# Decoder kernel on one core: reciprocal softmax sums transposed by DMA in 16-bit planes instead of on TensorE, and transposes moved in the slot order

## The chip, the core and the metric

The kernel runs on one core of one Trainium2 chip. The metric is the device time of one execution in microseconds; of three runs before the change the median is 2231.85 us (2231.59 to 2232.89). The trace comes from one further execution, taken with the hardware profiler.

The engines are named as the profile names them: PE is TensorE (PEld its weight loads), DVE is VectorE, ACT is ScalarE, POOL is GpSimd, SP is the queue from which nearly all DMAs are issued. Each engine executes its own instructions in order.

## What is computed

A decoder layer with post-norm, on 32 batches of 256 tokens by 256 features, all in float32 except the feed-forward matmuls. Cut to what matters here:

```python
x = layernorm(x + self_attn(x))          # 16 heads of 64, 4 KV heads, rope, alibi
x = layernorm(x + cross_attn(x, ctx))    # 16 heads of 16, windows of 64 keys, mask by cell
x = layernorm(x + ffn(x))                # 1024 wide, ternary weights, 8-bit activations

# inside self_attn
attn = softmax(q @ k.T / 8 + alibi)      # per head, 256 x 256
out  = (attn @ v).transpose(...).reshape(b, l, 16 * 64)
return out @ Wo
```

The change is inside the softmax of the self attention: its division by the row sums.

## The kernel before

**The unit of work.** One batch is cut into eight units of self scores (`self_units`: query half `qc`, KV half `kc`, head pair `rp`); two units make a pair, numbered m, with four pairs to a batch. A pair covers 128 queries and eight heads. For a pair:

- `self_scores` (L392, L408): PE writes scores to PSUM, DVE adds alibi, writes `p` and the row minimum `nm`.
- `self_exp` (L426): ACT takes exponentials in place and accumulates the row sums in `sums`, a [128 queries x 8 heads] tile.
- `self_turn` (L453, L458): PE transposes `p` in 128x128 blocks (as a matmul with `ident`), ACT copies them to `pT`.
- `self_values` (L470, L477): PE multiplies `v` with `pT`. The result `oT` has the 64 features of two heads on the partitions and the queries along the free axis; ACT copies it to SBUF. It is not normalized yet.
- `self_inverse` (L439, L441): DVE takes the reciprocals of `sums` and writes each one 64 times side by side in `wide`, [128 queries x 8 heads x 64].
- `self_spread` (L485): PE transposes `wide` in four 128x128 blocks to a PSUM bank `R`, so that each reciprocal stands on the 64 partitions of its head, over the queries.
- `self_normal` (L493): DVE multiplies `oT` by `R`.
- `self_output` (L501 and what follows): the output projection `wo`, the residual and the first layer norm, and the queries of the cross attention.

The cross attention has four units to a batch: `cross_scores` (L662, L676), `cross_exp` (L692), `cross_turn` (L701, L703: transposes `xp` on PE, ACT copies them to `xpT`), `cross_values` (L717, L726), `cross_back` (L737, L742, L743). The feed-forward has its own generator (L804 to L855).

**The order.** A hand-written schedule fixes the order on PE, DVE and ACT. Time is cut in slots, four to a pair: slot = 4m + part. In each slot the loop at the end of the kernel emits fixed pieces, and `parts()` emits the next piece of every generator that is due (projections of the coming batch, output projections, feed-forward, cross inputs). The cross attention runs CROSS = 4 pairs behind (k = m - 4). The order on SP and POOL isn't written by hand: the framework's scheduler places their instructions. In the text Q0, Q1, Q2 and Q3 are the four pairs m = 4b to 4b + 3 of a batch. The output projection of the first query half falls in Q2 (parts 1 and 2), that of the second in Q0; the feed-forward's gate matmuls fall in Q3 (parts 2 and 3), its up matmuls in Q0, its down matmuls in Q2.

**Buffers.** PSUM is a ring of eight banks (`bank`), taken in the order of the code; a matmul group waits until the bank that it takes, eight allocations back, has been read. SBUF tiles are taken from rings by name (`work(name, shape, bufs)`). SP's DMAs wait, in order, for their data: a DMA whose data is late holds those behind it. The DMAs on SP are rope's half swaps (`other<-psin`, `other<-qb`), loads of `xT`, `xs`, `cs`, `ck_i`, copies to `kTz` and `xvaug`, the store `out_dram<-x`, and the feed-forward's transposing DMAs `xiT` and `hiT` on bf16 data.

Of the kernel before, what the change touches and what calls it, by code (L numbers as in the profile page):

```python
# [9 lines left out]
F32 = mybir.dt.float32  # L10
BF16 = mybir.dt.bfloat16
I32 = mybir.dt.int32
AF = mybir.ActivationFunctionType
ALU = mybir.AluOpType
AX = mybir.AxisListType

P = 128
L = 256
NT = L // P
D = 256  # L20
NDC = D // P
# [4 lines left out]
H, KV, HD = 16, 4, 64  # L26
NCH = H // 2
# [23 lines left out]
def kernel(  # L51
# [27 lines left out]
    nc = tc.nc  # L79
# [5 lines left out]
    def ctile(shape, dtype, name):  # L85
        return const.tile(shape, dtype, name=name, tag=name)
# [3 lines left out]
    def bank(name, shape=(P, 512), dtype=F32):  # L90
        return ps.tile(list(shape), dtype, tag="b", name=name)


    ident = ctile([P, P], F32, "ident")
# [7 lines left out]
    def work(name, shape, bufs=2, dtype=F32):  # L102
        return sb.tile(list(shape), dtype, tag=name, name=name, bufs=bufs)

    def small(name, n):
        return sb.tile([P, 8], F32, tag="small", name=name, bufs=48)[:, 0:n]
# [21 lines left out]
    nc.scalar.dma_start(base_sb, mask_base)  # L128
    cq_i = ctile([P, B, NT], I32, "cq_i")
    nc.scalar.dma_start(cq_i, cell_q)  # L130
# [60 lines left out]
    def flush():  # L191
        while last:
            last.pop(0)()

    def scaled(dst, src, rb):

        nc.scalar.activation(dst, src, AF.Identity, bias=rb[:, 1:2], scale=rb[:, 0:1])

# [221 lines left out]
    def self_exp(b, i, half):  # L420
        s = state[b]
        p, nm = s["p", i][half], s.pop(("nm", i, half))
        for rr in range(2):
# [4 lines left out]
                p[:, cols],  # L428
                AF.Exp,
                bias=nm[:, rr : rr + 1],  # L430
# [3 lines left out]

    def self_inverse(b, m):

        s = state[b]
        rinv = small("rinv", 8)
        nc.vector.reciprocal(rinv, s.pop(("sums", m)))  # L439
        s["rinv", m] = wide = work("wide", [P, 8, HD], 1)  # L440
        nc.vector.tensor_copy(wide, rinv.unsqueeze(2).to_broadcast([P, 8, HD]))  # L441

    def self_turn(b, i):
        s = state[b]
# [31 lines left out]
                    )  # L476
        nc.scalar.copy(oT.rearrange("p c t -> p (c t)"), po)  # L477

    def self_spread(b, m):

        s = state[b]
        wide = s.pop(("rinv", m))
        s["R", m] = pr = bank("R")
        for r in range(NCH // 2):
            nc.tensor.transpose(  # L485
                pr[:, r * P : (r + 1) * P], wide[:, 2 * r : 2 * r + 2, :].rearrange("p a e -> p (a e)"), ident
            )

    def self_normal(b, m):
        s = state[b]  # L490
        qc, kc, _rp = self_units[2 * m]
        oT = s["oT", qc, kc].rearrange("p c t -> p (c t)")
        nc.vector.tensor_tensor(oT, oT, s.pop(("R", m)), ALU.mult)  # L493

    def self_output(b, qc):

        s = state[b]
        py = bank("wo")
        for kc in range(2):
            for r in range(NCH // 2):  # L500
                nc.tensor.matmul(  # L501
                    py[:, 0:D],
                    s["oT", qc, kc][:, r, :],
                    wo_sb[:, 4 * kc + r, :],
                    start=(kc == 0 and r == 0),
                    stop=(kc == 1 and r == 3),
                )
            if kc == 0:
                yield
        h = work("row", [P, D], 6)  # L510
        nc.vector.tensor_tensor(h, py[:, 0:D], s["xs"][:, qc, :], ALU.add)
        mv = stats(h, "x1")


        rs = small("rs_x1", 3)
        nc.gpsimd.tensor_scalar(rs[:, 0:1], mv[:, 1:2], EPS, None, ALU.add)
        nc.gpsimd.tensor_scalar(rs[:, 1:2], mv[:, 1:2], 1.0 + EPS, EPS * EPS, ALU.mult, ALU.add)
        nc.gpsimd.tensor_tensor(rs[:, 0:2], rs[:, 0:2], neg_half, ALU.pow)
        nc.gpsimd.tensor_scalar(rs[:, 2:3], mv[:, 0:1], rs[:, 0:1], -1.0, ALU.mult, ALU.mult)
        yield  # L520
        zq = work("row", [P, D], 6)

        s["x1", qc] = x1 = work("x1", [P, D], 4)

        def residual():
            nc.vector.tensor_scalar(zq, h, mv[:, 0:1], rs[:, 1:2], ALU.subtract, ALU.mult)
            nc.scalar.activation(x1, h, AF.Identity, bias=rs[:, 2:3], scale=rs[:, 0:1])
            nc.gpsimd.tensor_tensor(x1, x1, xbias[O_], ALU.add)

        last.append(residual)  # L530
        yield
        zqT = work("zT", [P, NDC, P])
        transposed(zqT, zq, "zqT")
        yield 2
        pq = bank("xq")
        for ch in range(NDC):
            for dc in range(NDC):
                nc.tensor.matmul(  # L538
                    pq[:, ch * P : (ch + 1) * P],
                    xq_w[:, dc, ch * P : (ch + 1) * P],  # L540
                    zqT[:, dc, :],
                    start=(dc == 0),
                    stop=(dc == NDC - 1),
                )
        s["xqT", qc] = work("xqT", [P, NDC, P])
        pair = biased(pq, Q_, P)
        yield 2
        rotated(s["xqT", qc], *pair, 0, qc * P)


    def biased(pq, j, n):


        qb = work("qb", [P, 2 * L])[:, 0 : NDC * n]
        for ch in range(NDC):
            nc.scalar.activation(
                qb[:, ch * n : (ch + 1) * n], pq[:, ch * n : (ch + 1) * n], AF.Identity, bias=xbcol[j][:, ch : ch + 1]
            )
        other = work("other", [P, 512], 3)[:, 0 : NDC * n]
        for e in range(2):  # L560
            nc.sync.dma_start(other[e : P : 2, :], qb[1 - e : P : 2, :])
        return qb, other
# [13 lines left out]
    def cross_inputs(b):  # L576
# [3 lines left out]
        nc.sync.dma_start(cs, cx[b].rearrange("(t p) d -> p t d", p=P))  # L580
        ck_i = work("ck_i", [P, L], 1, I32)
        nc.sync.dma_start(ck_i, cell_k[b].partition_broadcast(P))
# [104 lines left out]
    def cross_exp(b, i, half):  # L687
        s = state[b]
        p = s["xp", i, half]
        for j in range(XHH):  # L690
            cols = slice(j * P, (j + 1) * P)
            nc.scalar.activation(  # L692
                p[:, cols], p[:, cols], AF.Exp, bias=s["xnm", i][half][:, j : j + 1], scale=-1.0
            )
# [79 lines left out]
    def feed_forward(b):  # L774
# [39 lines left out]
        for t in range(NT):  # L814
            for half in range(2):
                pg = hidden("gate", t, half)
                cols = gu[:, t, half * 512 : (half + 1) * 512]
                nc.scalar.activation(cols, pg, AF.Tanh, scale=g_of[:, t : t + 1])  # L818
                nc.vector.scalar_tensor_tensor(cols, cols, 1.0, pg, ALU.add, ALU.mult)  # L819
# [48 lines left out]
    state = {b: {} for b in range(B)}  # L868
# [19 lines left out]
    with tc.manual_schedule(engines={mybir.EngineType.PE, mybir.EngineType.DVE, mybir.EngineType.Activation}):  # L888
        running = []
        slot = min(starts)  # L890
        while starts or running:
            m, part = divmod(slot, 4)
            k = m - CROSS
            for gen in starts.pop(slot, ()):
                running.append([slot, gen])

            def cross(f, unit, *more):
                if 0 <= unit < 4 * B:
                    f(*divmod(unit, 4), *more)

            def pair(f, unit):
                if 0 <= unit < 4 * B:
                    f(*divmod(unit, 4))

            def own(f, unit, *more):
                if 0 <= unit < 8 * B:
                    f(*divmod(unit, 8), *more)

            def parts():
                for r in list(running):  # L910
                    if r[0] == slot:
                        wait = next(r[1], r)
                        if wait is r:
                            running.remove(r)
                        else:
                            r[0] += wait or 1

            if part == 0:
                own(self_scores, 2 * m)
                own(self_scores, 2 * m + 1)  # L920
                own(self_exp, 2 * m, 0)
                own(self_exp, 2 * m, 1)
                own(self_exp, 2 * m + 1, 0)
                pair(self_values, m - 1)
                own(self_exp, 2 * m + 1, 1)
                pair(self_spread, m - 1)
                parts()
                pair(self_normal, m - 1)
                cross(cross_turn, k - 1, 0)
                cross(cross_turn, k - 1, 1)  # L930
            elif part == 1:
                parts()
                cross(cross_scores, k)
                cross(cross_values, k - 1)
                cross(cross_exp, k, 0)
            elif part == 2:
                parts()
                cross(cross_exp, k, 1)
                own(self_turn, 2 * m)
                cross(cross_back, k - 1)  # L940
            else:
                pair(self_inverse, m)
                parts()
                own(self_turn, 2 * m + 1)
            flush()
            slot += 1

# [88 lines left out]
```

## Time and profile before

| what | value |
|---|---|
| median of three runs | 2231.85 us |
| the profiled execution | 2230.19 us |
| its span | 2228.4 us |
| mean granted PE clock over the span | 0.986 |
| instructions | 55216 |
| DMA: bytes moved, mean | 144.05 MB, 65 GB/s |
| SP queue (q1), share of the 16 DMA engines' time | 24.6% |

The span is the profiled stretch; 1.8 us lie around it. The engine rows give busy time as a share of the span. A matmul's end is modelled, and matmuls overlap, so PE's busy share hides short waits: they are better seen from the starts of successive groups in the timeline. One batch is one period of the steady state; in the middle of the trace it lasts 66.48 us, from one start of Q0's value matmuls (1011.96 us) to the next (1078.44 us). Four stretches of this period begin with the value matmuls of a pair: Q0 at 1011.96, Q1 at 1026.95, Q2 at 1042.11, Q3 at 1064.06.

### The profile page before, as it was taken

How to read it: one execution, taken by the hardware profiler on the slowest of the kernel's cores; microseconds unless marked ns; L12 is line 12 of the kernel's file. 1: busy time of each engine (PE TensorE's matmuls, PEld its weight loads, DVE VectorE, ACT ScalarE, POOL GpSimd, SP SyncE). 2: the span in 40 equal slices, each digit the busy share in tenths (PEclk: the TensorE clock that was granted, in tenths of full speed). 3: DMA queues.
4: the chain of work that ended last, by engine and by line, in shares of the span. 5: the costliest groups of instructions: out<-in, count | busy, mean ns of one | idle time of the engine just before them, and what ended most of it. 6: DMA issues, size and time to landing. Idle time of an engine off the chain costs nothing.

```text
span 2228.4 us, 55216 instructions
## 1 busy us (share of the span) xinstructions
PE 2148.1 (96%) x17828; PEld 1672.0 (75%) x17828; DVE 1740.1 (78%) x6949; ACT 1678.0 (75%) x4961; POOL 1106.4 (50%) x1849
## 2 busy tenths in 40 slices
PE   7899999999999999999999999999999999999974
PEld 5687777777777777777777777777777777777752
DVE  4777888878887877887877887887788887888775
ACT  2577778887778877778787777887877887777862
POOL 4344554545554545544545544545555445555442
PEclk8999999999999999999999999999999999999996
DMA  6322222222222223222222322222222222222111
GB/s 206 94 57 56 69 55 63 62 56 70 70 54 62 64 55 73 68 57 63 61 58 70 69 59 58 60 64 65 70 66 53 66 58 63 70 63 49 34 41 31
DMA packets 191424, 144.05 MB, mean 65 GB/s; under 512 B 107808, under 2 KB 160928, under 8 KB 191136
## 3 DMA queue, kind: packets, MB, share of 16 engines
q1 hardware_dynamic: 189440, 136.95, 24.6%
q8 instruction: 142, 2.33, 0.5%
q10 hardware_dynamic: 1696, 3.57, 0.4%
q14 instruction: 146, 1.20, 0.2%
HBM read 39.50 MB, written 8.39 MB: 21 GB/s over the span
## 4 chain that ended last, share of the span: by engine, by line
PE 72%; DVE 11%; ACT 9%; issue 3%; DMA 2%; POOL 1%; SPq 1%; ACTq 0%; DVEq 0%; POOLq 0%
PE wo L501 10%; PE o L470 9%; PE proj L329 8%; PE t L453 8%; PE s L392 6%; PE ff L804 5%; ACT p L426 4%; PE xt L701 4%; PE xo L717 3%; PE xq L538 3%; PE xs L662 3%; PE ffo L851 3%; PE R L485 3%; PE xk L610 3%; PE xw L763 2%
## 5 line engine op out<-in xcount | busy, mean ns | idle before, releaser
L426 ACT ACTIVATE p<-p,nm 128x256 f32<-128x256 f32 x1024 | 507.3, 497 | 89.5 <-DVE nm L408 89.5
L458 ACT COPY pT<-t 128x512 f32<-128x512 f32 x512 | 275.9, 597 | 149.0 <-PE t L453 148.3
L408 DVE CUSTOM_DVE_ANT_0 p<-s,alibi 128x256 f32<-128x256 f32 x1024 | 361.9, 417 | 5.0 <-PE s L392 4.9
L692 ACT ACTIVATE xp<-xp,xnm 128x128 f32<-128x128 f32 x1024 | 327.2, 397 | 25.7 <-DVE xnm L676 25.7
L676 DVE CUSTOM_DVE_ANT_0 xp<-xs,mask 128x128 f32<-128x128 f32 x1024 | 225.8, 286 | 82.4 <-PE xs L662 82.1
L453 PE MATMUL t<-ident,p 128*128 128x128 f32 x2048 | 266.8, 273 | 0.9 <-ACT p L426 0.9
L470 PE MATMUL o<-pT,v 128*64 128x256 f32 x2048 | 261.0, 386 | 3.9 <-ACT pT L458 0.9
L453 PEld LDWEIGHTS t<-ident,p 128*128 128x128 f32 x2048 | 238.0, 141 | 27.0 <-ACT p L426 2.6
L353 POOL TENSOR_TENSOR qT<-qT,other 128x512 f32<-128x512 f32 x128 | 163.8, 1279 | 188.4 <-DMA other<-psin 138.7
L392 PE MATMUL s<-kT,qT 64*128 64x256 f32 x2048 | 255.7, 389 | 0.0
L329 PE MATMUL proj<-xT,wq_sb 128*128 128x256 f32 x1024 | 246.4, 385 | 0.0
L501 PE MATMUL wo<-wo_sb,oT 128*128 128x256 f32 x1024 | 245.3, 383 | 0.0
L470 PEld LDWEIGHTS o<-pT,v 128*64 128x64 f32 x2048 | 144.3, 136 | 106.7 <-issue 21.2
L392 PEld LDWEIGHTS s<-kT,qT 64*128 64x128 f32 x2048 | 187.9, 186 | 38.0 <-issue 16.1
L501 PEld LDWEIGHTS wo<-wo_sb,oT 128*128 128x128 f32 x1024 | 191.5, 192 | 27.0 <-DVE gu L297 0.3
L329 PEld LDWEIGHTS proj<-xT,wq_sb 128*128 128x128 f32 x1024 | 188.1, 193 | 21.7
L426 ACT ACTIVATION_READ_ACCUMULATOR p<-p,nm 128x1 f32 x1024 | 192.4, 188 | 0.0
L493 DVE TENSOR_TENSOR oT<-oT,R 128x512 f32<-128x512 f32 x128 | 86.9, 679 | 114.2 <-ACT oT L477 104.2
L840 POOL TENSOR_SCALAR gu<-gu,ffhup 128x1024 f32<-128x1024 f32 x64 | 72.8, 1137 | 161.3 <-DVE ffhup L836 161.3
L819 DVE SCALAR_TENSOR_TENSOR gu<-gu,ff 128x512 f32<-128x512 f32 x128 | 82.5, 684 | 77.2 <-ACT gu L818 77.2
L726 ACT COPY xoT<-xo 128x256 f32<-128x256 f32 x128 | 47.6, 372 | 124.9 <-PE xo L717 123.3
L600 POOL TENSOR_SCALAR mask<-ck_i,cq_sb 64x128 f32<-64x128 f32 (+1 forms) x96 | 70.2, 731 | 141.3 <-DVE xnm L676 135.3
(148 smaller groups left out, 4579.9 us busy)
## 6 DMA issues: line engine op xcount, KB each, us to landing
other<-psin SPq DMA_DIRECT2D x640, 64.0 KB, 2.0
xT<-in_xt_dram SPq DMA_DIRECT2D x32, 256.0 KB, 2.7
xs<-in_x_dram SPq DMA_DIRECT2D x32, 256.0 KB, 2.7
cs<-in_ctx_dram SPq DMA_DIRECT2D x32, 256.0 KB, 2.9
other<-qb SPq DMA_DIRECT2D x64, 128.0 KB, 2.0
kTz<-tr SPq DMA_DIRECT2D x256, 32.0 KB, 2.0
other<-qb SPq DMA_DIRECT2D x128, 64.0 KB, 1.9
out_dram<-x SPq DMA_DIRECT2D x32, 256.0 KB, 2.3
```

Of the source, the lines that this page charges most:

```text
L329: nc.tensor.matmul(pq[:, c * L : (c + 1) * L], w[:, dc, c * P : (c + 1) * P], xT[:, dc, :], start=(dc == 0), stop=(dc == NDC - 1),)
L353: nc.gpsimd.tensor_tensor(d2, d2, other, ALU.add)
L392: nc.tensor.matmul(banks[half][:, rr * L : (rr + 1) * L], qT[rows_, rr, qc * P : (qc + 1) * P], kT[rows_, kc, :], start=(rr == 0), stop=(r ...
L408: nc.vector.tensor_tensor_reduce(p[:, cols], banks[half][:, cols], alibi[:, 2 * (4 * kc + 2 * rp + rr) + half, :], -0.125, 3.0e38, ALU.add ...
L426: nc.scalar.activation(p[:, cols], p[:, cols], AF.Exp, bias=nm[:, rr : rr + 1], scale=-1.0, accum_out=s["sums", i // 2][:, e : e + 1],)
L453: nc.tensor.transpose(pt[:, j * P : (j + 1) * P], p[half][:, rr * L + kk * P : rr * L + (kk + 1) * P], ident,)
L458: nc.scalar.copy(pT[half], pt)
L470: nc.tensor.matmul(po[half * HD : (half + 1) * HD, rp * L : (rp + 1) * L], s["v"][:, kk, (2 * kc + half) * HD : (2 * kc + half + 1) * HD], ...
L501: nc.tensor.matmul(py[:, 0:D], s["oT", qc, kc][:, r, :], wo_sb[:, 4 * kc + r, :], start=(kc == 0 and r == 0), stop=(kc == 1 and r == 3),)
L676: nc.vector.tensor_tensor_reduce(p[:, cols], banks[2 * half + j // 2][:, j % 2 * P : (j % 2 + 1) * P], s["mask"][:, qc, :], -1.0, 3.0e38, ...
L692: nc.scalar.activation(p[:, cols], p[:, cols], AF.Exp, bias=s["xnm", i][half][:, j : j + 1], scale=-1.0)
L804: nc.tensor.matmul(pg, xiT[:, t, dc, :], ff_w[name][:, dc, half * 512 : (half + 1) * 512], start=(dc == 0), stop=(dc == NDC - 1),)
```

## The change

The reciprocals' transposition leaves PE. `self_inverse` now writes the reciprocals as 16-bit halves: a float32 is read as two uint16, and `wide` becomes [128, 2 planes, 8 heads, 64] uint16 (1024 elements for 512 before, the same bytes). A transposing DMA on SP, of 16-bit elements, turns it to `planes`. A new `self_spread` has POOL interleave the two planes back into float32 in an SBUF tile `R`; `self_normal` is unchanged in code but reads `R` from SBUF rather than PSUM. To make room, four rings are shortened: `row` from 6 to 4, `x1` from 4 to 3, `qb` from 2 to 1, and the new tiles have one buffer each.

The slot order changes too: `cross_turn` goes from the end of part 0 to directly behind `self_values`; `self_inverse` goes from the head of part 3 to part 2, ahead of `cross_exp(k, 1)` and `cross_back`; in part 3 `self_turn(2m + 1)` goes ahead of `parts()`; `self_spread` goes from part 0 of the next pair to the end of part 3.

```diff
     def self_inverse(b, m):
         s = state[b]
         rinv = small("rinv", 8)
         nc.vector.reciprocal(rinv, s.pop(("sums", m)))
-        s["rinv", m] = wide = work("wide", [P, 8, HD], 1)
-        nc.vector.tensor_copy(wide, rinv.unsqueeze(2).to_broadcast([P, 8, HD]))
+        wide = work("wide", [P, 2, 8, HD], 1, U16)
+        nc.vector.tensor_copy(
+            wide,
+            rinv.bitcast(U16).rearrange("p (a z) -> p z a", z=2).unsqueeze(3).to_broadcast([P, 2, 8, HD]),
+        )
+        s["planes", m] = planes = work("planes", [P, 2, NCH // 2, P], 1, U16)
+        nc.sync.dma_start_transpose(
+            planes.rearrange("p z r q -> p (z r) q"), wide.rearrange("p z a e -> p (z a e)")
+        )
+
+    def self_spread(b, m):
+        s = state[b]
+        s["R", m] = R = work("R", [P, 512], 1)
+        nc.gpsimd.tensor_copy(
+            R.bitcast(U16).rearrange("p (n z) -> p z n", z=2),
+            s.pop(("planes", m)).rearrange("p z r q -> p z (r q)"),
+        )
...
-    def self_spread(b, m):
-        s = state[b]
-        wide = s.pop(("rinv", m))
-        s["R", m] = pr = bank("R")
-        for r in range(NCH // 2):
-            nc.tensor.transpose(
-                pr[:, r * P : (r + 1) * P], wide[:, 2 * r : 2 * r + 2, :].rearrange("p a e -> p (a e)"), ident
-            )
...
-        h = work("row", [P, D], 6)
+        h = work("row", [P, D], 4)
...
-        zq = work("row", [P, D], 6)
-        s["x1", qc] = x1 = work("x1", [P, D], 4)
+        zq = work("row", [P, D], 4)
+        s["x1", qc] = x1 = work("x1", [P, D], 3)
...
-        qb = work("qb", [P, 2 * L])[:, 0 : NDC * n]
+        qb = work("qb", [P, 2 * L], 1)[:, 0 : NDC * n]
...
             if part == 0:
...
                 pair(self_values, m - 1)
+                cross(cross_turn, k - 1, 0)
+                cross(cross_turn, k - 1, 1)
                 own(self_exp, 2 * m + 1, 1)
-                pair(self_spread, m - 1)
                 parts()
                 pair(self_normal, m - 1)
-                cross(cross_turn, k - 1, 0)
-                cross(cross_turn, k - 1, 1)
...
             elif part == 2:
                 parts()
+                pair(self_inverse, m)
                 cross(cross_exp, k, 1)
                 own(self_turn, 2 * m)
                 cross(cross_back, k - 1)
             else:
-                pair(self_inverse, m)
+                own(self_turn, 2 * m + 1)
                 parts()
-                own(self_turn, 2 * m + 1)
+                pair(self_spread, m)
```

More of the change, by code (lines that the diff above doesn't have):

```diff
@@ L12 @@
 I32 = mybir.dt.int32
+U16 = mybir.dt.uint16
 AF = mybir.ActivationFunctionType
```

## The prediction

> **What bounds the kernel now.** I read the page first: engine shares, slices and the chain that ended last.
>
> ```profile
> PE 2148.1 (96%) x17828; PEld 1672.0 (75%) x17828; DVE 1740.1 (78%) x6949; ACT 1678.0 (75%) x4961; POOL 1106.4 (50%) x1849
> ...
> PE   7899999999999999999999999999999999999974
> ...
> PE 72%; DVE 11%; ACT 9%; issue 3%; DMA 2%; POOL 1%; SPq 1%; ACTq 0%; DVEq 0%; POOLq 0%
> ```
>
> PE is nearly always busy, and POOL half idle, so taking work from PE and giving it to POOL looks right. But a fifth of the chain is on DVE and ACT: in places PE is not the limit. Second, the timelines of one period, first PE, then ACT and DVE around the start of Q0:
>
> ```profile
> 1009.85 2.00 PE L392 MATMUL s<-kT,qT 64*128 64x256 f32 x16
> 1011.96 2.33 PE L470 MATMUL o<-pT,v 128*64 128x256 f32 x16
> 1014.22 0.66 PE L485 MATMUL R<-ident,wide 128*128 128x128 f32 x4
> 1014.71 1.03 PE L763 MATMUL xw<-xo_w,zT 128*128 128x256 f32 x4
> ...
> 1026.95 1.95 PE L470 MATMUL o<-pT,v 128*64 128x256 f32 x16
> ```
>
> ```profile
> 1009.51 1.09 ACT L458 COPY pT<-t 128x512 f32<-128x512 f32 x2
> 1010.45 1.31 ACT L818 ACTIVATE gu<-ff,ffg 128x512 f32<-128x512 f32 x2
> 1011.60 1.12 ACT L458 COPY pT<-t 128x512 f32<-128x512 f32 x2
> 1012.94 0.51 ACT L426 ACTIVATE p<-p,nm 128x256 f32<-128x256 f32 x1 [0.22 <-DVE nm L408]
> ```
>
> ```profile
> 1011.22 1.28 DVE L819 SCALAR_TENSOR_TENSOR gu<-gu,ff 128x512 f32<-128x512 f32 x2 [0.50 <-ACT gu L818]
> ```
>
> In Q1 and Q2 each PE group starts where the last ends: `o` takes 1.95 us. From Q3 to the start of Q0 ACT works without a gap, and PE waits for it: `o` in Q0 takes 2.33 us and starts 0.17 us after `s` has let go (1009.85 + 1.93 = 1011.79), about 0.55 us lost. Busy times by stretch agree: ACT is busy 13.20 of Q3's 14.38 us, but 12.04 of Q0's 14.99.
>
> **The change, part by part.**
>
> *R leaves PE.* A run of eight transposes lasts 0.87 us in the chain of waits, so four cost 0.44 us. The R group holds PE 0.49 us to the next start, and 0.59 in the chain; the rest is a pause at the change from 64-column to 128-column weights (the weight loads of R sit idle 0.38 us before it, put down to issue), which the next 128-column group, `xt`, will pay instead. So 128 pairs x 0.44 = 56 us of PE time go; upper end 128 x 0.59 = 76.
>
> *DVE's `wide`.* The row of before, and those that price its successor:
>
> ```profile
> L441 DVE COPY wide<-rinv 128x512 f32<-128x512 f32 x128 | 84.9, 664 | 4.4
> L843 DVE TENSOR_SCALAR hib<-gu 128x1024 bf16<-128x1024 f32 x64 | 44.3, 693 | 10.1 <-POOL gu L840 10.1
> ```
>
> Now 1024 elements are written for 512. `hib` writes 1024 in 0.69 us; the old `wide` takes 0.43 undisturbed (426 ns its minimum). I take 0.69, +0.27 a pair; lowest +0 (all halves packed), highest +0.8, from the 1024-element reduction L831 at 1.21 us. DVE has room except before `s` in Q3, below. `oT` times R (0.69 us) keeps its size; reading R from SBUF may make it wait for POOL, as `wide` does (up to 1532 ns): between 0 and +0.8, taken 0.
>
> *The transposing DMA.* It has the size and form of `hiT`:
>
> ```profile
> hiT<-hib SPq DMA_TRANSPOSE x64, 3.1
> ```
>
> so 1.28 us on SP and 3.1 us to landing, 128 times: 164 us more of SP, which idles much. Here a rule speaks against the change: the Trainium skill, "VectorE: DVE Perf Modes", section "The three transpose paths", gives 390 ns for a 128x128 16-bit block on TensorE and 1309 ns by DMA, and its rules keep TensorE wherever PSUM output will do. Estimated from that page, four blocks (1.56 us) are exchanged for eight (10.5 us), a clear loss. The rows are far from both: 0.44 us of PE for 3.1 us of latency. What decides is that the one is PE's time and the other only delay, if R still arrives.
>
> *POOL's spread.* 1024 two-byte elements, one input. Nearest row: the same operation on `ck_i`, 256 elements in 0.40 us; with the slope of one-input work on POOL (L840, 1024 elements, 1.14; L791, 256, 0.48: 0.86 ns an element) that gives 1.06 us. Upper end: the slowest one-input row of POOL, L223 at 922 ns for 256, would make 3.7. I take 1.1 (nearest in kind). It adds 136 us to POOL's 1106.
>
> *Does R come in time?* On SP and POOL the new order sets it. Each case starts from `wide`, in times of before, and ends at L493, which can't start before ACT's copy of `oT`:
> - Q0's (wide 1024.5): SP idle, landed 1027.7; POOL has `x1` and half of `rstd_zo` ahead (1027.5); R at 1028.8, L493 at 1030.6.
> - Q1's (1040.8 to 1041.2): landed 1044.5; POOL first finishes `xqT` (1045.5); R 1046.6, L493 1047.7.
> - Q2's (1060.4): its DMA now stands behind the store `out_dram`, which waits for ACT's last `x` (1062.8 before, about 1060 once the fourth slot's transposes come first); landed 1064; POOL ends rope and `x1` at 1065.3; R 1066.4, L493 1068.8.
> - Q3's (about 1076.5): the DMA is put between the `kTz` copies, landed 1079.6; R 1080.7, L493 about 1083.
>
> So R is 1.1 to 2.4 us early. Behind Q3's DMA wait five `kTz` copies (0.67 us each, 2.0 to landing): done near 1083, and `xs` of Q0 needs them at 1084.2. Behind Q1's stand the second `hiT` and rope swaps, used some 8 us later or about 1 us late for POOL, which has nothing urgent there. `rstd_zo` behind R comes 1.1 us later, used by ACT 4 us on.
>
> *Head.* In the first pair POOL's R stands behind `ck_i` and the mask (done 50.3 us), while L493 ran at 47.1: DVE waits 4.3 us. It idles 6.3 us at 60 to 66, waiting in the end for ACT and POOL, so part is absorbed: cost 0 to 4, taken 2.
>
> *`cross_turn` earlier.* ACT now makes the `xpT` copies ahead of two exponentials (2 x 0.49) and `zT` (0.25): `xo` gets its data 1.2 us sooner, `zT` comes at the time of the old `xpT`; `xq`, behind `xo`, then waits for that in Q3. *Fourth slot's transposes earlier.* PE no longer waits at Q0's `o`: gain 0.55 at that place. But in Q3 ACT's second pair of tanh now follows both copies, so DVE's `gu` and the scores behind it come later. *Rings.* `qb` is read by POOL to 1064.6, its next writer is at 1072.9; 1045.5 against 1055.1 in the other case; `row` and `x1` turn over slots apart: no cost. If POOL were 8 us late, ACT would stand at `qb`.
>
> *Sum for one batch.* The path that sets Q3 and Q0: `wo` ends at 1056.8 on PE, DVE works without a gap to the scores of Q3, ACT starts its exponentials at 1065.19 and goes on to Q0's `xo` (1085.4). On it: wide +0.27; behind the copies, tanh to 1079.5, `gu` and one score to 1080.6, so exponentials 1.2 later than 1079.4; then six instead of eight of them ahead of `xpT`: -0.98. `xpT` is ready at 1085.1, `xo` gains 0.3 us where PE alone would gain 1.9. Q1 and Q2 are bound by PE and gain 0.44 each. Together 1.2 us x 32 batches = 38 us; head +2. Profiled execution: 2230.2 (span 2228.4 and 1.8 around it) - 36 = 2194; the median stands 1.7 above it: **2195 us**.
>
> **The rivals.**
> - *PE sets the whole period.* For it: 96% busy, no visible wait in most groups; if DVE's scores in Q3 aren't held by `gu` the 56 us are all real, and with the 0.55 at Q0's `o` (18 us): 2232 - 72 = 2160. Against: ACT's unbroken row from Q3 on.
> - *R comes too late: slower.* Place: L493, in order on DVE, with the whole of part 1 behind it. Price: if POOL's spread takes t, R misses L493 in Q1 from t = 2.2 us on, in Q0 from 2.9, in Q2 from 3.4. At the upper end of 3.7 these are 1.5, 0.8 and 0.3, 2.6 us a batch on DVE; less the 1.2 gained, 1.4 x 32 = 45: about 2277. The sign turns near t = 3.1. Against it: no one-input row of POOL in the steady state is that slow for its size. A `kTz` landing late at Q0's `xs` is milder, 1 us x 32, and would leave 2227.
> - *Nothing moves.* The pause at the weight change and ACT's path eat the gain: within 5 us.
>
> **Chances and range.** Likeliest (2180 to 2215): 0.48. PE-bound (2150 to 2180): 0.26. Nothing: 0.06. Slower: 0.20. A measurement of this kernel tells 0.2% (4.5 us) from no change. Faster 0.74, same 0.06, slower 0.20. The range 2152 to 2245 leaves out the larger part of the slower case and the tail of the faster one; the likeliest's own is 2180 to 2215.
>
> **What would show it.** No L485; `wide` near 690 ns; a DMA row `planes` near 3.1 us; the POOL copy near 1.1 us; L493 still waiting for ACT's `oT`, not for POOL. A period of about 65.3 us, `xo` of Q0 waiting for `xpT`, and ACT waiting over 1 us at Q0's first exponential. Wrong if L493 waits for POOL's R in most pairs, if `xs` waits for `kTz`, or if POOL's copy is above 2.2 us.

## The result, and the profile after

After the change the median of four runs is **2210.83 us** (2209.87 to 2211.08), beside 2231.72 us of four runs before (2230.14 to 2232.89): a ratio of **0.9906** [0.9889, 0.9923], 20.9 us less. The profiled execution took 2211.1 us, with a span of 2209.3 us at a mean granted clock of 0.980 (0.986 before; the undisturbed PE groups keep their times, `wo` 1.73 us in both).

From the page of the changed kernel, busy times and the chain that ended last:

```profile
PE 2103.3 (95%) x17254; PEld 1617.7 (73%) x17316; DVE 1789.9 (81%) x6949; ACT 1659.5 (75%) x4961; POOL 1316.8 (60%) x1977
...
PE 58%; DVE 20%; ACT 12%; DMA 3%; issue 2%; POOL 1%; SPq 0%; ACTq 0%; POOLq 0%; DVEq 0%
```

PE does 44.8 us less, but the span is only 19.1 us shorter. PE's share of the chain fell from 72 to 58%, DVE's rose from 11 to 20%, ACT's from 9 to 12%: where PE made room, the other two now end last. The view of waits names the places (total us, times, longest):

```profile
ACT p L427 <- DVE nm L409: 235.8, 94, 21.9
...
DVE oT L500 <- ACT oT L494: 110.2, 120, 2.8
...
PEld xq L545 <- ACT zT L205: 51.6, 63, 1.1
...
PE xq L545 <- ACT zT L205: 37.8, 61, 0.8
...
DVE oT L500 <- POOL R L455: 9.6, 3, 4.5
```

ACT's exponentials on the page of before, with 89.5 us of waiting ahead of them:

```profile
L426 ACT ACTIVATE p<-p,nm 128x256 f32<-128x256 f32 x1024 | 507.3, 497 | 89.5 <-DVE nm L408 89.5
```

ACT waits 235.8 us for DVE's scores, where it waited 89.5 us before. The wait of `xq` for `zT` is new: 61 times, two a batch. `oT` times `R` still waits for ACT's `oT`; for POOL's `R` it does so only three times, two of them in the first 200 us (7.9 us, the longest 4.5).

The timeline of PE (start, us) from Q3 to Q1 of one batch:

```profile
993.95 1.42 PE L669 MATMUL xs<-kTz,xqT 32*64 32x256 f32 x16
995.30 0.79 PE L724 MATMUL xo<-xpT,xvaug 128*32 128x64 f32 x32
996.92 1.16 PE L545 MATMUL xq<-zT,xq_w 128*128 128x128 f32 x8 [0.82 <-ACT zT L205]
...
1001.91 2.49 PE L393 MATMUL s<-kT,qT 64*128 64x256 f32 x16
1004.33 1.95 PE L487 MATMUL o<-pT,v 128*64 128x256 f32 x16
...
1024.00 0.64 PE L724 MATMUL xo<-xpT,xvaug 128*32 128x128 f32 x16
1025.06 1.16 PE L545 MATMUL xq<-zT,xq_w 128*128 128x128 f32 x8 [0.41 <-ACT zT L205]
```

Before, in Q1:

```profile
1032.88 0.64 PE L717 MATMUL xo<-xpT,xvaug 128*32 128x128 f32 x16
1033.46 1.16 PE L538 MATMUL xq<-zT,xq_w 128*128 128x128 f32 x8
```

No `R` stands between `o` and `xt` any more, and `o` of Q0 takes 1.95 instead of 2.33 us. Three things are longer: `xq` in Q3 stands 0.82 us, `s` of Q0 takes 2.49 instead of 2.00, and `xq` in Q1, which followed `xo` at once before, stands 0.41 us. A busy row of digits hides all three. To sum them, take the time from one PE group's start to the next, averaged over 20 batches in the middle of the run (us; four of the experiments below stand beside it). `s` of Q0 is the score group ahead of Q0's `o`:

| step of PE | before | after | moves alone (e3) | e3 without `R` (e5) | 512 float32 `wide` (e9) | 1024 16-bit `wide` (e10) |
|---|---|---|---|---|---|---|
| `R` and `xt`, four pairs | 5.46 | 3.72 | 5.47 | 3.72 | 3.72 | 3.72 |
| Q3: `xs` | 1.13 | 1.02 | 0.72 | 0.75 | 0.72 | 0.94 |
| Q3: `xo`, up to `xq` | 0.84 | 1.61 | 1.05 | 1.55 | 1.51 | 1.61 |
| Q0: `s` | 2.10 | 2.42 | 2.04 | 2.04 | 2.42 | 2.42 |
| Q0: `o` | 2.26 | 1.88 | 1.88 | 1.88 | 1.88 | 1.88 |
| Q0: `xs` and `xo` | 1.23 | 1.24 | 1.24 | 1.63 | 1.24 | 1.24 |
| Q1: `xo`, up to `xq` | 0.57 | 1.06 | 0.57 | 0.64 | 0.81 | 1.07 |
| period of a batch | 66.45 | 65.85 | 65.86 | 65.11 | 65.16 | 65.78 |

From before to after: -1.74 for `R`, -0.11, +0.77, +0.32, -0.38 and +0.49 in the rows below it, together -0.65, and 0.05 more at Q2's `xs`; the period fell by 0.60, and 32 x 0.60 = 19 us. So of 1.74 us that left PE in each batch, about 1.1 came back: at `xq` as waits for ACT's `zT`, at `s` of Q0 in part as waits for ACT's `pT` (29 waits of its weight loads, one in nearly every batch).

The pieces of the transport, by form (busy us, mean ns | idle us before, releaser), and its DMA beside one of the same form:

```profile
L455 POOL COPY R<-planes 128x1024 uint16<-128x1024 uint16 x128 | 173.5, 1356 | 21.9 <-DMA planes<-wide 21.6
...
L443 DVE COPY wide<-rinv 128x1024 uint16<-128x1024 uint16 x128 | 108.2, 845 | 4.5 <-DVE rinv L441 0.2
...
L533 DVE TENSOR_SCALAR row<-row,mv_x,rs_x 128x256 f32<-128x256 f32 x64 | 50.3, 785 | 1.2 <-POOL rs_x L525 1.1
```

```profile
planes<-wide SPq DMA_TRANSPOSE x128, 3.1
...
hiT<-hib SPq DMA_TRANSPOSE x64, 3.1
```

`wide` is 693 ns at its least, 798 in the median and 1445 at its longest. The DMA lands after 3.1 us, as its neighbour does. `row<-row`, which the change doesn't touch, has a mean of 0.82 us in the middle of the run, against 0.60 before: this row is the clue to what follows.

### The profile page after: what moved, and what is told of

Read it like the earlier page. It is cut to its first block, busy times and chain, and to the rows that moved or that the text cites. A ratio compares the mean times of both kernels' runs of the same rounds, so it can differ in the third digit from the quotient of the medians.

```text
span 2209.3 us, 54605 instructions
## 1 busy us (share of the span) xinstructions
PE 2103.3 (95%) x17254; PEld 1617.7 (73%) x17316; DVE 1789.9 (81%) x6949; ACT 1659.5 (75%) x4961; POOL 1316.8 (60%) x1977
## 3 DMA queue, kind: packets, MB, share of 16 engines
q8 instruction: 138, 2.26, 0.4%
q14 instruction: 150, 1.23, 0.2%
## 4 chain that ended last, share of the span: by engine, by line
PE 58%; DVE 20%; ACT 12%; DMA 3%; issue 2%; POOL 1%; SPq 0%; ACTq 0%; POOLq 0%; DVEq 0%
PE wo L508 9%; PE t L470 8%; DVE p L409 7%; PE s L393 6%; ACT p L427 6%; PE o L487 5%; PE proj L330 5%; PE ff L811 4%; PE xq L545 3%; PE xt L708 3%; ACT xpT L710 3%; PE ffo L858 3%; PE xk L617 2%; PE xw L770 2%; PE v L362 2%; DMA out_dram<-x 2%
## 5 line engine op out<-in xcount | busy, mean ns | idle before, releaser
L427 ACT ACTIVATE p<-p,nm 128x256 f32<-128x256 f32 x1024 | 508.3, 499 | 235.8 <-DVE nm L409 235.8
L393 PE MATMUL s<-kT,qT 64*128 64x256 f32 x2048 | 271.4, 392 | 0.0
L475 ACT COPY pT<-t 128x512 f32<-128x512 f32 x512 | 263.7, 598 | 7.0 <-PE t L470 6.8
L354 POOL TENSOR_TENSOR qT<-qT,other 128x512 f32<-128x512 f32 x128 | 178.7, 1396 | 137.9 <-DMA other<-psin 113.1
L487 PE MATMUL o<-pT,v 128*64 128x256 f32 x2048 | 249.8, 386 | 0.0
L393 PEld LDWEIGHTS s<-kT,qT 64*128 64x128 f32 x2048 | 197.5, 187 | 68.6 <-issue 16.2
L487 PEld LDWEIGHTS o<-pT,v 128*64 128x64 f32 x2048 | 136.4, 137 | 98.1 <-issue 42.3
L500 DVE TENSOR_TENSOR oT<-oT,R 128x512 f32<-128x512 f32 x128 | 98.0, 765 | 119.8 <-ACT oT L494 110.2
L455 POOL COPY R<-planes 128x1024 uint16<-128x1024 uint16 x128 | 173.5, 1356 | 21.9 <-DMA planes<-wide 21.6
L847 POOL TENSOR_SCALAR gu<-gu,ffhup 128x1024 f32<-128x1024 f32 x64 | 73.5, 1149 | 143.9 <-DVE ffhup L843 143.9
L708 PEld LDWEIGHTS xt<-ident,xp 128*128 128x128 f32 x1024 | 112.1, 143 | 49.0 <-issue 36.2
```

What stands on the lines that cost most here:

```text
L354: nc.gpsimd.tensor_tensor(d2, d2, other, ALU.add)
L393: nc.tensor.matmul(banks[half][:, rr * L : (rr + 1) * L], qT[rows_, rr, qc * P : (qc + 1) * P], kT[rows_, kc, :], start=(rr == 0), stop=(r ...
L427: nc.scalar.activation(p[:, cols], p[:, cols], AF.Exp, bias=nm[:, rr : rr + 1], scale=-1.0, accum_out=s["sums", i // 2][:, e : e + 1],)
L475: nc.scalar.copy(pT[half], pt)
L487: nc.tensor.matmul(po[half * HD : (half + 1) * HD, rp * L : (rp + 1) * L], s["v"][:, kk, (2 * kc + half) * HD : (2 * kc + half + 1) * HD], ...
L708: nc.tensor.transpose(pt[:, j * P : (j + 1) * P], p[:, j * P : (j + 1) * P], ident)
```

## The experiments

The theory to be tested (A) is this: from Q3 to Q0 ACT's row of work, fed by DVE's scores, sets the time, so time won on PE there returns as a wait. Against it: PE still sets the period and one of the moves does harm; or a part of the transport, `wide`, the DMA or POOL's copy, costs the time. All ratios are to the kernel before, run on the same chip.

| run | what | us | ratio [95%] | period, us |
|---|---|---|---|---|
| e1_cross_back | after, `cross_turn` at its old place | 2257.33 | 1.0104 [1.0089, 1.0120] | 67.29 |
| e2_turn_back | after, fourth slot's `self_turn` at its old place | 2204.53 | 0.9866 [0.9852, 0.9881] | 65.55 |
| e3_moves_only | before, with both moves; `R` stays on PE | 2208.06 | 0.9880 [0.9865, 0.9895] | 65.86 |
| e4_parts_first | after, `parts()` of part 0 ahead of `cross_turn` | 2206.96 | 0.9875 [0.9858, 0.9891] | 65.59 |
| e5_no_r_moved | e3 without `R` | 2185.81 | 0.9799 [0.9785, 0.9814] | 65.11 |
| e6_no_r_before | before without `R` | 2203.51 | 0.9878 [0.9863, 0.9893] | 65.53 |
| e7_no_pool_copy | after without POOL's copy | 2207.30 | 0.9898 [0.9881, 0.9914] | 65.78 |
| e8_cross_only | before, with the move of `cross_turn` alone | 2224.55 | 0.9970 [0.9959, 0.9981] | 66.37 |
| e9_wide32_early | after without DMA and copy, `wide` in float32 | 2190.70 | 0.9804 [0.9788, 0.9819] | 65.16 |
| e10_wide16_only | e9 with the 16-bit `wide` | 2208.50 | 0.9888 [0.9874, 0.9903] | 65.78 |
| e11_r_on_pe_parts_first | e3 with `R` and `parts()` ahead of `cross_turn` | 2208.41 | 0.9889 [0.9872, 0.9905] | 65.81 |
| e12_turn_back_parts_first | after with the edits of e2 and e4 | 2207.46 | 0.9883 [0.9868, 0.9897] | 65.63 |

The medians of before beside them were 2233.53 (e1 to e4), 2230.67 (e5 to e8) and 2232.09 us (e9 to e12). e5, e6, e7, e9 and e10 multiply `oT` by ones in place of `R`, so the softmax isn't normalized in them; DVE's multiplication keeps its size, but not its time: its mean over the 20 batches is 0.81 us in e5 and 0.84 in e6, beside 0.69 in e3 and 0.68 before; in e7, e9 and e10 it is 0.73, beside 0.75 in after.

**The move of `cross_turn`, undone and alone.** e1, against after:

```diff
                 pair(self_values, m - 1)
-                cross(cross_turn, k - 1, 0)
-                cross(cross_turn, k - 1, 1)
                 own(self_exp, 2 * m + 1, 1)
                 parts()
                 pair(self_normal, m - 1)
+                cross(cross_turn, k - 1, 0)
+                cross(cross_turn, k - 1, 1)
```

> The changed kernel with cross_turn back at the end of part 0. In the changed kernel the query matmuls xq wait for ACT's zT copy in Q1 (0.49 us a batch) and Q3 (0.77). Theory A (ACT's row from the scores on is the limit; the order only chooses which copy is last): xpT becomes the last copy, xo waits in place of xq, and xq, which follows xo, starts some 0.3 us later in each of the two: period 66.2 to 66.5 us, time 2217 to 2232. Theory B (the waits are made by the move of cross_turn alone): both waits go, period 64.6 us, time near 2171.

Measured: 1% slower than before, 67.29 us a batch, worse than either theory had it, although nothing stands on PE for `R`. Its PE timeline, `xo` of Q3, Q0 and Q1:

```profile
1014.10 0.91 PE L724 MATMUL xo<-xpT,xvaug 128*32 128x64 f32 x32 [1.06 <-ACT xpT L710]
...
1029.05 0.91 PE L724 MATMUL xo<-xpT,xvaug 128*32 128x64 f32 x32 [0.62 <-ACT xpT L710]
...
1043.43 0.91 PE L724 MATMUL xo<-xpT,xvaug 128*32 128x128 f32 x16 [0.52 <-ACT xpT L710]
```

`xo` waits three times in each batch for copies that ACT makes behind all eight exponentials. So this move is no ornament: beside the rest of the change the old place of `cross_turn` costs 1.44 us a batch (65.85 to 67.29). It isn't `R`'s absence alone that makes it so dear: e6 below, the old order throughout without `R`, is faster than before.

e8 makes the same move in the kernel before, and nothing else:

> The kernel before with one move alone: cross_turn directly behind self_values; R stays on PE, the fourth slot keeps its order. If the gain of the change is this move: period 65.5 to 65.9, time 2197 to 2210. If it needs R off PE or the other move: 66.2 or more, 2222 or more.

It gains 0.3%, some 6 us, as if the move needed `R` off PE or the other move. `xo` is free and `xs` in Q3 0.46 us shorter, but the step from `xo` to `xq` is 0.19 longer (1.03), `s` of Q0 takes 2.29 us (2.10 before), and `o` keeps its 2.26.

**Both moves, with `R` left on PE.** e3, against before:

```diff
                 pair(self_values, m - 1)
+                cross(cross_turn, k - 1, 0)
+                cross(cross_turn, k - 1, 1)
                 own(self_exp, 2 * m + 1, 1)
...
-                cross(cross_turn, k - 1, 0)
-                cross(cross_turn, k - 1, 1)
...
                 pair(self_inverse, m)
-                parts()
                 own(self_turn, 2 * m + 1)
+                parts()
```

> The kernel before, with R on PE, and only the two moves: cross_turn directly behind self_values, fourth slot's transposes ahead of parts(). Theory A: the moves trade the waits at xo and o (0.26 and 0.55 us a batch) for one at xq (0.4 to 0.8): period 66.2 to 66.5, time 2223 to 2234. Theory D (the moves are worth what the forecast gave them, 0.5 us or more a batch): time 2212 or less.

Both moves are `cross_turn`'s and the fourth slot's; `self_inverse` stays where it was. Measured: 0.9880, and the period of the whole change to 0.01 us; that is theory D's outcome, not A's. So the two moves alone bring what the change brings, with 1.75 us of `R` still on PE. The table has both columns: after has no `R`, and pays 0.30 and 0.56 in Q3, 0.38 at `s` of Q0 and 0.49 in Q1, together 1.73.

**`R` taken away for nothing.** e5 removes `R` from e3, without a transport; e6 removes it from before. The edit in both:

```diff
-        nc.vector.tensor_tensor(oT, oT, s.pop(("R", m)), ALU.mult)
+        o3 = s["oT", qc, kc]
+        nc.vector.tensor_tensor(o3, o3, ones.unsqueeze(1).to_broadcast([P, NCH // 2, P]), ALU.mult)
...
-                pair(self_spread, m - 1)
```

> Both moves on the kernel before, R nowhere: wide is written in float32 as before, PE's four transposes of it are left out, there is no DMA and no POOL copy, and oT is multiplied by ones (the normalization is left out). Theory H (PE's time under R lies beside ACT and DVE, which set the end; leaving it out makes PE wait longer): period 65.4 to 65.9, time 2195 to 2210, waits at xo, xq and Q0's s larger than with R on PE by about what went. Theory T (R's place on PE is worth 1.7 us a batch and the transport gives it back through DVE and POOL): period 64.1 to 64.6, time 2155 to 2172.

> The kernel before in its own order, R nowhere: as the run above but without the moves (the normalization is left out). Theory H: xpT is the last copy of ACT's row and PE now waits for it at xo in Q3, Q0 and Q1; period 65.9 to 66.4, time 2215 to 2230. Theory T: period 64.7, time near 2176.

In the moved order the period falls by 0.75 us (65.86 to 65.11), in the old order by 0.92 (66.45 to 65.53), where PE loses some 1.7 us of work. Both lie between the two theories: of PE's 56 us, 24 to 29 came out by the periods (18 and 27 by the ratios), and the rest stayed hidden behind other engines. DVE's longer multiplication (four times 0.13 to 0.16 us a batch) may hide some of it, so what a removal at no cost at all would bring isn't shown. But a PE that set the whole period would have given 56. That answers this rival, and leaves a question: the change keeps none of those 0.75 us.

**Which part of the transport takes them?** e7 leaves out POOL's copy alone (the multiplication as in e5):

```diff
             else:
                 own(self_turn, 2 * m + 1)
                 parts()
-                pair(self_spread, m)
```

> The changed kernel with the 16-bit wide and its transposing DMA, but without POOL's copy; oT is multiplied by ones (the normalization is left out). Theory H: as the changed kernel, period 65.7 to 65.9, time 2205 to 2212. Theory T, in the form that POOL's 1.35 us copies hold up DVE's [...]instructions before the scores (row, xib, wide): those shrink to the times of before and the period falls by the 0.6 us by which Q3's scores are late, to 65.2 or less, time 2190 or less.

The period is 65.78 us, 0.07 less than after: the copy, 1.35 us on POOL 128 times, is worth some 2 us of the whole at most (0.9898 and 0.9906 have overlapping intervals). e9 also leaves out the DMA, and writes `wide` in float32 as before; e10 differs from e9 in one instruction:

```diff
-        wide = work("wide", [P, 8, HD], 1)
-        nc.vector.tensor_copy(wide, rinv.unsqueeze(2).to_broadcast([P, 8, HD]))
+        wide = work("wide", [P, 2, 8, HD], 1, U16)
+        nc.vector.tensor_copy(
+            wide,
+            rinv.bitcast(U16).rearrange("p (a z) -> p z a", z=2).unsqueeze(3).to_broadcast([P, 2, 8, HD]),
+        )
```

> The changed kernel's order and rings, with wide in float32 as before and R nowhere: no PE transposes, no DMA, no POOL copy, oT times ones (the normalization is left out). It differs from the run with both moves and no R (period 65.11) by self_inverse in part 2 and the shorter rings. If these cost the 0.7 us a batch that the changed kernel lies above that run: period 65.7 or more, time near 2205. If the 16-bit wide and its DMA cost it: 65.1, time near 2186.

> As the run above, but with the 16-bit wide of 1024 elements (the normalization is left out; no DMA, no POOL copy). If the longer DVE instruction is the cost (0.2 us in each pair, two of them ahead of the scores of Q3 and Q1): period 65.6 to 65.8, time 2202 to 2208. If the transposing DMA is: period as in the run above.

e9 is at 65.16 us (so the shorter rings and the earlier `self_inverse` cost only 0.05 against e5, though they take the late data from Q0's `xs` and `xo` to `s` of Q0 and Q1's `xq`), e10 at 65.78, the same as e7, which has the DMA too. **The DMA costs nothing that these runs can tell, and one DVE instruction costs 0.62 us a batch, 18 us in all.** Its own length explains it only in part: four times 0.27 us are spread over a batch, and can be absorbed, as Q1 shows. The two timelines show how it reaches the scores in Q1. DVE in e9, from the reciprocals to the first score:

```profile
1005.68 0.17 DVE L441 RECIPROCAL rinv<-sums 128x8 f32<-128x8 f32 x1
1005.89 0.43 DVE L443 COPY wide<-rinv 128x512 f32<-128x512 f32 x1
...
1007.05 1.28 DVE L827 TENSOR_TENSOR gu<-gu,ff 128x512 f32<-128x512 f32 x2 [0.30 <-PE ff L806]
...
1008.81 0.57 DVE L528 TENSOR_SCALAR row<-row,mv_x,rs_x 128x256 f32<-128x256 f32 x1
1009.30 0.41 DVE L409 CUSTOM_DVE_ANT_0 p<-s,alibi 128x256 f32<-128x256 f32 x1
```

The same in e10:

```profile
1013.33 0.17 DVE L441 RECIPROCAL rinv<-sums 128x8 f32<-128x8 f32 x1
1013.54 0.70 DVE L443 COPY wide<-rinv 128x1024 uint16<-128x1024 uint16 x1
...
1014.71 1.29 DVE L830 TENSOR_TENSOR gu<-gu,ff 128x512 f32<-128x512 f32 x2
...
1016.47 0.82 DVE L531 TENSOR_SCALAR row<-row,mv_x,rs_x 128x256 f32<-128x256 f32 x1
1017.21 0.41 DVE L409 CUSTOM_DVE_ANT_0 p<-s,alibi 128x256 f32<-128x256 f32 x1
```

POOL beside them, first e9, then e10:

```profile
1005.85 0.50 POOL L518 TENSOR_SCALAR rs_x<-mv_x 128x1 f32<-128x1 f32 x1 [3.85 <-DVE rinv L441]
...
1008.50 0.72 POOL L530 TENSOR_TENSOR x<-x,xbias 128x256 f32<-128x256 f32 x1 [0.72 <-ACT x L529]
```

```profile
1013.51 0.77 POOL L521 TENSOR_SCALAR rs_x<-mv_x 128x1 f32<-128x1 f32 x1 [3.04 <-DVE rinv L441]
...
1016.42 0.72 POOL L533 TENSOR_TENSOR x<-x,xbias 128x256 f32<-128x256 f32 x1 [0.72 <-ACT x L532]
```

Count from the reciprocals; the times of one batch are given, and all 20 in the middle have the same pattern. The 0.27 us of `wide` itself are absorbed: `gu` starts 1.37 us later in e9, after a wait of 0.30 for PE, and 1.38 us later in e10, without one. But POOL's first `rs_x`, which starts with `wide`, ends 0.03 or 0.04 us behind it (1006.35 against 1006.32; 1014.28 against 1014.24), so it takes 0.77 us instead of 0.50. POOL's chain, ACT's `x` and POOL's `x<-x,xbias` come 0.27 us later behind it (3.09 instead of 2.82), and DVE's `row<-row`, which starts at 3.13 or 3.14, ends 0.15 us behind that `x` in both. So it takes 0.82 us instead of 0.57, and the first score comes at 3.88 instead of 3.62. Those 0.26 us are the 0.26 that the table shows at `xq` in Q1 (0.81 to 1.07): scores, exponentials and `zT` pass them on to PE (the first exponential of Q1, counted from `xk`, goes from 40.09 to 40.67 us, of which 0.32 are PE's own delay since Q3). The Trainium skill ("SBUF — State Buffer", section "SBUF: two separate sides") says that DVE, in an operation that uses both of its ports, and GpSimd exclude each other for a whole instruction. These ends agree with it; but a `row<-row` of 0.38 us at its least ends only 0.15 us after POOL's, so at least 0.23 us of it passed beside POOL's operation, as far as POOL's spans can be trusted.

In Q3 the first exponential comes 0.32 us later in e10 than in e9 (12.50 against 12.18 us after `xk`), and PE's `xs` and `xo` are 0.22 and 0.10 longer. There `wide`, `xib` (from a mean of 0.72 to 1.04 us) and `row<-row` are all stretched ahead of the scores; which of the three decides was not separated.

**The fourth slot's transposes, and `parts()`.** e2, against after:

```diff
-                own(self_turn, 2 * m + 1)
                 parts()
+                own(self_turn, 2 * m + 1)
                 pair(self_spread, m)
```

> The changed kernel with the fourth slot's transposes behind parts() again. Theory A (ACT is the limit from Q3 to Q0): PE waits at Q0's o once more (0.38 us a batch), Q0's first exponential comes about 1 us sooner, the wait at Q0's s (0.49) stays or shrinks: period 65.8 to 66.2, time 2210 to 2223. Theory C (the move delays gu, the scores and so all of Q0 and Q1): without it Q1's wait of xq goes too, period 65.3, time near 2195.

Measured: 0.9866, the fastest here that normalizes; 65.55 us a batch, between the two theories. ACT's wait for the scores falls to 107.6 us (235.8 in after). `o` of Q0 takes 2.13 us, near its old 2.26 (theory A), but `xq` in Q1 no longer waits (0.57; theory C). In Q1 the long `wide` does no harm here:

```profile
1015.37 0.38 DVE L533 TENSOR_SCALAR row<-row,mv_x,rs_x 128x256 f32<-128x256 f32 x1
```

```profile
1015.45 0.89 POOL L535 TENSOR_TENSOR x<-x,xbias 128x256 f32<-128x256 f32 x1 [0.72 <-ACT x L534]
```

The reciprocals start at 1012.36, and POOL's `x` comes 3.09 us behind them as in e10, but `row<-row` starts first, at 3.01 instead of 3.14. It keeps its 0.38 us, POOL's operation takes 0.89 instead of 0.72, and the first score comes at 3.30 instead of 3.88.

So this move, worth 0.51 us a batch beside `R` on PE (e8 to e3), costs 0.30 beside the transport. e4 moves `parts()` in part 0:

```diff
                 pair(self_values, m - 1)
+                parts()
                 cross(cross_turn, k - 1, 0)
                 cross(cross_turn, k - 1, 1)
                 own(self_exp, 2 * m + 1, 1)
-                parts()
                 pair(self_normal, m - 1)
```

> The changed kernel with parts() of part 0 ahead of cross_turn and of the last two exponentials, so that ACT makes zT first, then xpT, then the exponentials. Theory A (ACT sets Q3 and Q0, PE sets Q1 and Q2): xq's wait in Q1 goes (-0.49), that in Q3 goes too but comes back as a longer wait at Q0's s: period 65.3 us, time near 2195. Theory B (zT's place in ACT's order is the only loss): both go, period 64.6, time near 2171.

`xq` waits nowhere (0.83 in Q3, 0.57 in Q1), yet the period falls by 0.26 only, less than either theory gave: `xs` in Q3 rises to 1.22, the second `t` ahead of Q0 from 0.87 to 1.20, `s` of Q0 from 2.42 to 2.72. That is theory A in its kind, though not in its size: in Q3 and Q0 a wait that is taken away comes back in another group. Two more orders were tried for a better version:

> R on PE, both moves, and parts() of part 0 (with R ahead of it) in front of cross_turn and the last two exponentials, so that zT no longer waits for them on ACT. In the run with both moves xq waits 0.47 us for zT in Q3. If that is all: period 65.4 to 65.6, time 2192 to 2200. If ACT's row sets Q3 and Q0 in any order, the wait moves to Q0's s: 65.8, time 2206.

> The changed kernel with both single improvements so far: fourth slot's transposes behind parts() again (period 65.55 alone) and parts() of part 0 ahead of cross_turn (65.59 alone). If they add: 65.3, time near 2196. If both give the same wait back at Q0's s: 65.5 to 65.6, time 2203 to 2208.

Neither is one: 2208.41 and 2207.46 us, where each expectation had the wait come back. The gains of e2 and e4 don't add up. e2, e3, e4, e11 and e12 lie within 4 us of each other and their intervals overlap; e2 lies 0.4% below after, each set against the kernel before of its own chip.

## Why the prediction was right and wrong

It forecast 2195 us, from 1.2 us a batch; the period fell by 0.6. The direction and the mechanism of Q3 and Q0 hold, ACT's row being last; the 0.3 us there came out by luck, and Q1 failed.

- *R leaves PE, 0.44 us a pair.* Right: `R` and `xt` took 1.36 us and take 0.93, 0.43 less. The pause at the change of weights went to `xt`, as foreseen.
- *Q3 and Q0 gain 0.3 together.* Right in size: two pairs of `R` (-0.87), -0.11, +0.77, +0.32 and -0.38 make -0.27. But this is two misses that cancel. The sum names `wide`'s +0.27 on this path and adds no term for it (`xpT`'s end before, 1084.9, + 1.2 - 0.98 = 1085.1); by the same rows the path gains 0.67 with the short `wide` (e9) and 0.35 with the long one (e10). Wrong in place: the late data were to show at `xo` of Q0 (0.59, no wait), and they show at `xq` of Q3, behind `zT`, and at `s` of Q0, behind `pT`. With `self_inverse` at its old place (e5) Q0's `xs` and `xo` do take 0.39 us more. ACT's wait at Q0's first exponential is there: 1.18 us in one batch, over 1 foreseen.
- *"Q1 and Q2 are bound by PE and gain 0.44 each."* **This is the step that failed.** Q2 gained 0.43, less 0.05 at `xs`. Q1 gained 0.43 and lost 0.49 at `xq`: 32 x 0.49 = 15.7 us, about all of the 15.8 us by which the forecast was too low. The premise was "DVE has room except before `s` in Q3". It has none before the scores of Q1 either, where ACT starts as soon as they come. Of the 0.49 us, 0.07 come with the freed PE time (e3 to e5), 0.17 with the earlier `self_inverse` and the shorter rings, which no run separates (e5 to e9), and 0.26 with the longer `wide`, by way of POOL (e9 to e10). All of it goes with the turn's move: e2, with the same transport but the old turn, pays nothing.
- *`wide`, +0.27.* Right for the instruction: 0.70 against 0.43. The lower end, +0, was the case in which all halves are packed. The Trainium skill ("VectorE: DVE Perf Modes", section "The perf-mode tier table") has 693 ns for a copy of 2048 16-bit elements at four a cycle; at two a cycle 1024 take the same number of cycles, so by that rule 693 ns are the estimate, and 693 is the minimum measured. What was missed is its neighbour: POOL's `rs_x` ends 0.04 us behind it at either length, and POOL stands in DVE's way later.
- *The transposing DMA, only delay.* Right: 1.26 us on SP, 3.1 to landing, no cost (e10 and e7 both at 65.78). The estimates that were weighed against the change, 10.5 us by DMA for 1.56 on TensorE, are far from what was measured: eight blocks landed after 3.1 us, and four float32 ones took PE 0.44. Whether TensorE is the better place stays open: with `R` on PE (e3) and off it (e2, e4) the times differ by less than their intervals.
- *POOL's copy, 1.1 us.* It takes 1.35 (1.32 ns an element, not the 0.86 of the slope), and costs at most 0.07 us a batch, off the path. `R` is in time, as worked out; `kTz` is late once, by 0.6 us. In the head the longest wait is 4.5 us, 4.3 foreseen.
- *The moves, worth the 0.55 at Q0's `o` and an earlier `xpT`.* Undervalued. The sum gave most of the gain to `R`; the moves alone bring all of it (e3). `R` taken away for nothing would bring 0.75 us more, and its transport, with the earlier `self_inverse` and the shorter rings, costs as much (65.11 to 65.85). That the total fell into the likeliest range while its parts were wrong was luck, and no profile of after alone could have told it.

The rivals: PE as the bound of the whole period falls with e5, where the removal without a transport gives 24 us. `R` too late falls with three waits in 128. Nothing moving falls with the interval.

## What to carry to other kernels

An engine that is 96% busy need not be the bound: price its work by the step from one group's start to the next, and ask at each such step who was last, because work taken off it can come back as waits wherever another engine's row ends at the same time. Before work is moved to idle engines, look at the one instruction that feeds it on a busy engine: here the latency of the DMA and of POOL was hidden, and a copy 0.27 us longer ate 0.62 of the 0.75 us. When a change both moves and replaces, run the moves alone.

## What was not expected of the hardware

- Writing the same 2 KB a partition as 1024 16-bit halves from a repeated source takes DVE 0.70 us, as 512 float32 0.43.
- DVE's and POOL's operations stretch each other: `wide` takes up to 1445 ns from 693, `rs_x` 0.50 us beside the short `wide` and 0.77 beside the long one (0.21 in the median), and an untouched `row<-row` a mean of 0.69 us in e9 and 0.82 in e10.
- Of `row<-row` and POOL's `x` in Q1, which start within 0.1 us of each other, the first keeps its time and the second takes longer: 0.38 and 0.89 us in e2, where DVE is first by 0.08; 0.82 and 0.72 in e10, where POOL is first by 0.05. The first score comes 0.58 us earlier in e2.
- A copy on POOL that interleaves two 16-bit planes costs 1.32 ns an element; its float32 row of the same size (L847, 1149 ns) 1.12.
